# The seam between two layers: the last block's norm, its residuals, and the tensors and pools that layer 1 waits for

## The chip, the core and the metric

The kernel runs on one core of one Trainium2 chip. Its time is the device time of one execution in microseconds (us). The engines named here are PE (TensorE: matmuls, and PEld, its weight loads), DVE (VectorE), ACT (ScalarE), POOL (GpSimd) and SP (SyncE, which only issues DMAs). Each engine works through its own instructions in order and waits on semaphores for the others. A DMA is issued from SP's, POOL's or ACT's queue and lands later.

## The reference

Two residual layers on x of shape (4, 64, 256, 256), float32. `_gn` is a group norm of 32 groups without weights.

```python
    def _L0_conv_ref(x, w1, w_dw, w_out, ln_w, ln_b):
        hidden = jnp.einsum('bchw,oc->bohw', x, w1)
        hidden = jax.lax.conv_general_dilated(hidden, w_dw, window_strides=(1, 1), padding='SAME', feature_group_count=w_dw.shape[0], dimension_numbers=('NCHW', 'OIHW', 'NCHW'))
        q, k, v = jnp.split(hidden, 3, axis=1)
        qf = jnp.fft.rfft2(_to_patches(q))
        kf = jnp.fft.rfft2(_to_patches(k))
        out = jnp.fft.irfft2(qf * kf, s=(P, P))
        ...
        mu = out.mean(axis=1, keepdims=True)
        var = out.var(axis=1, keepdims=True)
        out = (out - mu) / jnp.sqrt(var + 1e-05) * ln_w[None, :, None, None] + ln_b[None, :, None, None]
        out = v * out
        return jnp.einsum('bchw,oc->bohw', out, w_out)

    def _L1_conv_ref(features, w_ih, w_hh, b_ih, b_hh):
        ...
        def step(prev_col, cur_col):
            nb = jnp.concatenate([pad, prev_col, pad], axis=1)
            x = jnp.concatenate([nb[:, :-2], nb[:, 1:-1], nb[:, 2:]], axis=-1)
            new = _gru_cell(x.reshape(B * H, 3 * Cf), cur_col.reshape(B * H, Cf), w_ih, w_hh, b_ih, b_hh).reshape(B, H, Cf)
            return (new, new)
        ...

    x = x + _L0_conv_ref(_gn(x), L0_conv_w1, L0_conv_w_dw, L0_conv_w_out, L0_conv_ln_w, L0_conv_ln_b)
    x = x + _L1_conv_ref(_gn(x), L1_conv_w_ih, L1_conv_w_hh, L1_conv_b_ih, L1_conv_b_hh)
```

Layer 0 mixes 8x8 patches by a circular convolution of q and k, takes a layer norm over the channels, multiplies with v and projects back. Layer 1 is a recurrence from image column to image column: a GRU cell whose input is the last column and whose state is the current one. Its group norm needs statistics over the whole of layer 0's result.

## The kernel before

Layer 0 goes through the image in `NBLK` = 32 blocks (line 617), eight to an image, each of 32 columns of the transposed image: block n belongs to image n // 8 and to columns 32 * (n % 8) to 32 * (n % 8) + 31. A block runs in stages: the pointwise product into `h` for one chunk of channels (16 units), `circular` (transform, products, inverse into `z`), a second chunk and `circular`, a third chunk, and `values` (k = 0 to 7, into `v`). The matrices `t` of the transforms are streamed from DRAM on SP's queue through four buffers (`fetch`, line 334). TensorE's results pass through a ring of eight PSUM banks (`psum`, line 220).

What follows on a block (norm, gate, projection, residual) is done beside the next block's TensorE work. `layer_norm` (line 472) is a generator, moved on by `go()`: statistics of `z` on DVE, the standard deviation on ACT, then eight scalings of `z` on DVE (`scaled`, for four slices of 32 features a subtraction of the mean and a multiplication with its reciprocal deviation), then eight transposes on DVE, of `z` and `v` by turns (`turned`). `gated` (line 527) takes one slice of 32 features: weight and bias of the norm on ACT, the product with `v` on POOL. `project(n, u)` (line 551) multiplies half u of the pixels with `w_out` on TensorE, four groups b of which each needs one slice. `residual(n, u)` (line 540) loads the matching part of x from DRAM to `wk` slots 6 and 2 with four DMAs on SP's queue, `add_residual` adds on DVE, and `leave` (line 579) takes statistics (`bn_stats`, after half 1 also the aggregate into `st1`) on DVE and stores the result to the DRAM tensor `x1` with four DMAs on POOL's queue.

For the last block there is no next one. At `n == NBLK` (line 620) the generator runs to its end, the four slices are gated, and for each half in turn come residual, project, add and leave. Both halves use the same slots of `wk`, so half 1's load waits for half 0's stores.

Then layer 1 begins. Its constants go to a pool `l1c` (line 730). `norm_of_blocks` (line 109) makes four means and deviations from `st1`, with two small matmuls for the sums over channels, in a short-lived pool `stb`; from them comes `sc1` (line 745), in two layouts, for even and odd columns. `load_column(w)` (line 773) loads column w of `x1` for all images to one of 16 buffers `raw`; 16 columns are loaded ahead on SP's queue. `normalize(w, slot)` of layer 1 (line 787) makes `xn` from `raw` and `sc1` on ACT and a copy `xt` with the halves exchanged on POOL. Eight of these, for columns 0 to 3, stand ahead of the first column's matmuls, and POOL then clears the edges of the state tile `st`, which the first taps read.

Pools of layer 0 lie in this order: `xp` (four buffers `xq`), `big` (`h`, `z`, `v`, `wk` and small tiles), `tp` (four `t`). They are given back when layer 0 ends, and layer 1's pools lie where they lay. A new pool's first use waits for the old one's last. Every instruction passes through one helper (`InOrder.run`, line 158), so the profile's line is L158 for nearly all; the groups are told apart by tiles and shapes.

Of the kernel before, what the change touches and what calls it, by code (L numbers as in the profile page):

```python
# [9 lines left out]
F32 = mybir.dt.float32  # L10
# [98 lines left out]
def norm_of_blocks(nc, tmp, pool, psum, mv, eps, avg4):  # L109
# [3 lines left out]
    mean = pool.tile([P, NPAIR], F32, tag="gn1_mean", name="gn1_mean")  # L113
    rstd = pool.tile([P, NPAIR], F32, tag="gn1_rstd", name="gn1_rstd")
    m_all = tmp.tile([P, NBLK], F32, tag="m_all", name="m_all")
    d = tmp.tile([P, NBLK], F32, tag="d_all", name="d_all")
    m4 = tmp.tile([P, B], F32, tag="m4", name="m4")
    nc.vector.tensor_copy(m_all, mv[:, :, 0])
    nc.vector.tensor_reduce(
        m4, m_all.rearrange("p (b n) -> p b n", n=n), mybir.AxisListType.X, ALU.add  # L120
# [6 lines left out]
        m_all.rearrange("p (b n) -> p b n", n=n),  # L127
# [5 lines left out]
    v4 = tmp.tile([P, B], F32, tag="v4", name="v4")  # L133
# [4 lines left out]
    nc.vector.reciprocal(v4, v4)  # L138
    for b in range(B):
        at = slice((b % 2) * C, (b % 2) * C + C)  # L140
        nc.vector.tensor_copy(mean[at, b // 2 : b // 2 + 1], m4[at, b : b + 1])
        nc.vector.tensor_copy(rstd[at, b // 2 : b // 2 + 1], v4[at, b : b + 1])
    return mean, rstd
# [20 lines left out]
def tile_conv_then_gru(  # L164
# [20 lines left out]
    x1 = dram.tile([B, C, W, H], F32, tag="x1", name="x1")  # L185
# [27 lines left out]
    with layer0 as s:  # L213
        big = s.enter_context(tc.tile_pool(name="big", bufs=1))
# [11 lines left out]
        hx = big.tile([P, P * NP], F32, tag="h", name="h")  # L226
# [245 lines left out]
        def layer_norm(n):  # L472
# [31 lines left out]
            def scaled(i):  # L504
                f = slice(32 * i, 32 * i + 32)
                for part, what in ((mean, ALU.subtract), (rstd, ALU.mult)):
                    nc.vector.tensor_tensor(
                        z[:, :, f],
                        z[:, :, f],
                        part.rearrange("p (n x) -> p n x", x=1).to_broadcast([P, NJ, 32]),  # L510
                        what,
                    )
                    yield

            def turned(of, i):
                chunk = of[:, :, 32 * i : 32 * i + 32]
                nc.vector.transpose(chunk, chunk)

            for i in range(4):
                yield from scaled(i)  # L520
            for i in range(4):
                turned(z, i)
                yield
                turned(v, i)
                yield

        def gated(n, i):
            f = slice(32 * i, 32 * i + 32)
            nc.scalar.activation(
                z[:, :, f],  # L530
                z[:, :, f],
# [4 lines left out]
            nc.gpsimd.tensor_tensor(v[:, :, f], v[:, :, f], z[:, :, f], ALU.mult)  # L536
# [3 lines left out]
        def residual(n, u):  # L540
            b, r0 = n // 8, (n % 8) * 32 + u * 8
            xr = [wk[:, i].rearrange("p (r c) -> p r c", c=P) for i in (6, 2)]
# [36 lines left out]
        def leave(n, u, xr):  # L579

            b, r0 = n // 8, (n % 8) * 32 + u * 8
            if u == 0:
                bn[n] = big.tile([P, 8, 6], F32, tag="bn", name=f"bn_{n}")
            for g in range(2):
# [3 lines left out]
                for s in range(2):  # L588
                    nc.gpsimd.dma_start(
                        x1[b, :, r0 + 16 * g : r0 + 16 * g + 8, s * P : s * P + P],  # L590
# [26 lines left out]
        for n in range(NBLK + 1):  # L617
            last = n == NBLK
            more = not last and n // 8 + 1 < B
            if last:  # L620
                for _ in norm:
                    pass
                for i in range(4):
                    gated(n - 1, i)
                for u in range(2):
                    xr = residual(n - 1, u)
                    add_residual(u, project(n - 1, u), xr)
                    leave(n - 1, u, xr)
# [54 lines left out]
            for unit in range(16):  # L683
# [13 lines left out]
                if unit % 4 == 3 and n + 1 < NBLK:  # L697
                    load(n + 1, unit // 4)
            po = project(n - 1, 1) if n else None
# [4 lines left out]
            for k in range(8):  # L704
# [12 lines left out]
                if k == 5 and n:  # L717
                    leave(n - 1, 1, xr[1])
                if k == 5 and n + 1 < NBLK:
                    normalize(n + 1, 3)  # L720
                if k in (6, 7):
# [18 lines left out]
    with tc.tile_pool(name="stb", bufs=1) as stb, tc.tile_pool(name="gnps1", bufs=1, space=PSUM) as gnps:  # L740
        avg4 = stb.tile([P, P], F32, tag="avg4", name="avg4")
        nc.scalar.dma_start(avg4, avg2)
        mean1, rstd1 = norm_of_blocks(nc, stb, l1c, gnps, st1, eps, avg4)
# [231 lines left out]
```

## Time and profile before

| what | value |
|---|---|
| median of 3 runs | 5094.03 us |
| lowest and highest | 5087.31, 5103.36 us |
| the profiled execution's own time | 5097.92 us |
| its span | 5096.1 us |
| mean granted TensorE clock | 0.993 |
| DVE, ACT, POOL busy | 79%, 65%, 34% of the span |
| layer 0's last values (PE) begin | 3657.29 us |
| layer 1's first tap matmul | 3735.32 us |

A row of the timeline gives start, duration, engine, line, operation, what it writes and reads, partitions x elements and, in brackets, the engine's idle time before it and what ended it. Rows of equal kind that follow each other are put together (x4). Consecutive instructions of one engine can overlap a little at their ends.

### The profile page before, as it was taken

What the parts mean: (1) busy time and instruction counts of PE and PEld (TensorE: products, weight loads), DVE (VectorE), ACT (ScalarE), POOL (GpSimd) and SP (SyncE); (2) the same over time, 40 slices, a digit from 0 to 9 for tenths busy, and PEclk for the clock granted to TensorE, in tenths of its full rate; (3) what the DMA queues carried; (4) which work ended last, traced back from release to release, by engine and by line L of the source; (5) the groups of instructions that cost most, each with busy time, mean ns of one, the idle gap of its engine ahead of it and who ended that gap; (6) DMA issues with size and microseconds to landing.
All of it is one profiled execution on the core that took longest, in us unless ns stands there. A gap on an engine that the chain in (4) does not pass through costs nothing.

```text
span 5096.1 us, 276113 instructions
## 1 busy us (share of the span) xinstructions
PE 4858.1 (95%) x127092; PEld 4237.7 (83%) x127092; DVE 4035.9 (79%) x7001; ACT 3317.3 (65%) x4269; POOL 1727.2 (34%) x1717
## 2 busy tenths in 40 slices
PE   6999999999999999999999999999879999999999
PEld 4888888888888888888888888888669999999998
DVE  5788888877888888788888877778867777777777
ACT  4666666666666666666666666666556666666665
POOL 0233333333333334333333333323343333333333
PEclk9999999999999999999999999999989999999999
DMA  8577676676777667677676666666443333333332
GB/s 306 162 189 191 186 191 182 180 183 187 187 195 196 170 184 187 179 190 191 186 195 168 173 161 174 173 171 180 121 125 103 104 103 103 102 104 103 103 103 73
DMA packets 435056, 823.57 MB, mean 162 GB/s; under 512 B 37156, under 2 KB 300068, under 8 KB 431364
## 3 DMA queue, kind: packets, MB, share of 16 engines
q1 hardware_dynamic: 380600, 582.13, 43.3%
q0 software_dynamic: 52432, 223.12, 14.7%
q8 instruction: 997, 16.33, 1.4%
q14 instruction: 163, 1.34, 0.1%
q10 hardware_dynamic: 864, 0.66, 0.0%
HBM read 660.53 MB, written 145.23 MB: 158 GB/s over the span
## 4 chain that ended last, share of the span: by engine, by line
PE 87%; ACT 4%; issue 4%; DVE 3%; DMA 2%; POOL 1%; SPq 0%; POOLq 0%; ACTq 0%; DVEq 0%
PE psring L158 62%; PE pshr L158 9%; PE pshz L158 8%; PE psni L158 6%; PE pshn L158 2%; ACT v L158 1%; ACT z L158 1%; DVE wk L158 1%; ACT xq L158 1%; DMA t<-t_all 1%; DVE z L158 1%; DMA t_all<-wk 0%; DVE lnst L158 0%; ACT h L158 0%; POOL v L158 0%
## 5 line engine op out<-in xcount | busy, mean ns | idle before, releaser
L158 PEld LDWEIGHTS psring<-h,t 100*32 100x32 f32 x49152 | 1385.9, 119 | 251.6 <-issue 214.5
L158 PE MATMUL psring<-h,t 100*32 100x128 f32 x49152 | 1463.5, 257 | 104.2 <-issue 69.4
L158 PEld LDWEIGHTS psring<-w_sb,xq 64*100 64x100 f32 x24576 | 1358.6, 163 | 107.9 <-issue 76.5
L158 PE MATMUL psring<-w_sb,xq 64*100 64x128 f32 x24576 | 1412.4, 271 | 23.0 <-issue 8.7
L158 ACT COPY h<-psring 100x1024 f32<-100x1024 f32 (+2 forms) x1371 | 1231.5, 990 | 308.0 <-PE psring L158 307.4
L158 DVE TENSOR_TENSOR wk<-psring,wk 128x1024 f32<-128x1024 f32 (+1 forms) x768 | 759.5, 1037 | 480.1 <-PE psring L158 346.4
L158 POOL TENSOR_TENSOR v<-v,z 128x2048 f32<-128x2048 f32 x128 | 582.9, 4558 | 664.5 <-DVE wk L158 603.5
L158 DVE TENSOR_TENSOR z<-z,moments 128x2048 f32<-128x2048 f32 x256 | 578.0, 2278 | 2.3
L158 POOL TENSOR_TENSOR wk<-wk 128x1024 f32<-128x1024 f32 x128 | 303.5, 2371 | 622.3 <-DVE wk L158 607.9
L158 POOL TENSOR_TENSOR raw<-raw,st 128x512 f32<-128x512 f32 x256 | 303.2, 1184 | 540.1 <-DVE st L158 424.6
L158 ACT COPY z<-psring 128x2048 f32<-128x2048 f32 (+1 forms) x144 | 248.4, 1725 | 343.9 <-PE psring L158 262.6
L158 ACT ACTIVATE z<-pshz,b_rz 128x288 f32<-128x288 f32 (+7 forms) x510 | 242.1, 475 | 339.2 <-PE pshz L158 334.1
L158 ACT COPY wk<-psring 128x1024 f32<-128x1024 f32 (+1 forms) x272 | 268.9, 988 | 288.5 <-PE psring L158 237.1
L158 PE MATMUL pshr<-st,wi 64*64 64x144 f32 (+7 forms) x12240 | 448.8, 270 | 6.9 <-DVE st L158 6.5
L158 PE MATMUL pshz<-st,wi 64*64 64x144 f32 (+7 forms) x12240 | 444.2, 269 | 0.9 <-issue 0.9
L158 PE MATMUL psni<-st,wi 64*64 64x144 f32 (+7 forms) x12240 | 444.0, 269 | 0.1
L158 DVE COPY h<-psring 100x1024 f32<-100x1024 f32 (+1 forms) x230 | 278.1, 1210 | 191.9 <-PE psring L158 188.1
L158 PEld LDWEIGHTS pshr<-st,wi 64*64 64x64 f32 x12240 | 378.0, 133 | 49.7 <-DVE st L158 36.9
L158 ACT COPY v<-psring 128x2048 f32<-128x2048 f32 (+2 forms) x176 | 251.9, 1436 | 254.3 <-PE psring L158 254.3
L158 DVE BATCH_NORM_STATS2 lnst<-z 128x6 f32<-128x128 f32 x2048 | 416.8, 281 | 0.0
L158 PEld LDWEIGHTS psni<-st,wi 64*64 64x64 f32 x12240 | 389.4, 133 | 21.9 <-issue 0.2
L158 PE MATMUL psring<-wk,g_sb 32*64 32x512 f32 x6144 | 386.7, 599 | 15.1 <-issue 12.1
(91 smaller groups left out, 6258.4 us busy)
## 6 DMA issues: line engine op xcount, KB each, us to landing
t<-t_all SPq DMA_DIRECT2D x768, 448.0 KB, 4.6
xq<-in_xh POOLq DMA_DIRECT2D x124, 800.0 KB, 5.2
wk<-in_x SPq DMA_DIRECT2D x256, 256.0 KB, 8.1
x<-wk POOLq DMA_DIRECT2D x256, 256.0 KB, 5.0
wk<-in_x POOLq DMA_DIRECT2D x96, 512.0 KB, 6.9
raw<-x SPq DMA_DIRECT2D x128, 256.0 KB, 3.0
raw<-x SPq DMA_DIRECT2D x256, 128.0 KB, 3.1
out<-raw SPq DMA_DIRECT2D x128, 256.0 KB, 2.7
```

The costliest lines, as they stand in the source:

```text
L158: return self.tc.keep_in_program_order(got(*args, **kwargs))
```

## The change

The last block's norm is shared: `scaled` takes an engine, and slices 2 and 3 of block 31 are scaled on POOL, slices 0 and 1 on DVE. Its transposes go by halves of the pixels (32 of 64), its gates too, and each half is projected once its four slices are gated; the product of the last slice of half 1 is on DVE. Both halves are added, then both leave. The residuals of block 31 are loaded beside block 31's own third chunk: half 0 to `wk` slots 1 and 5, half 1 to slots 6 and 2 after block 30's last stores, which go out on SP's queue instead of POOL's. The generator isn't moved on at k = 6 and 7 of the last block. `x1` becomes eight DRAM tensors of 32 columns each. `h` gets a pool of its own, `hp`, between `xp` and `big`. `norm_of_blocks` uses tiles of `l1c` in place of `stb`, leaves out a copy and builds `sc4` for all images at once, from which four copies make `sc1`; a Sigmoid of one element per partition follows its Sqrt on ACT.

```diff
-def norm_of_blocks(nc, tmp, pool, psum, mv, eps, avg4):
+def norm_of_blocks(nc, tmp, psum, mv, eps, avg4, sc):
...
     n = NBLK // B
-    mean = pool.tile([P, NPAIR], F32, tag="gn1_mean", name="gn1_mean")
-    rstd = pool.tile([P, NPAIR], F32, tag="gn1_rstd", name="gn1_rstd")
-    m_all = tmp.tile([P, NBLK], F32, tag="m_all", name="m_all")
     d = tmp.tile([P, NBLK], F32, tag="d_all", name="d_all")
     m4 = tmp.tile([P, B], F32, tag="m4", name="m4")
-    nc.vector.tensor_copy(m_all, mv[:, :, 0])
+    v4 = tmp.tile([P, B], F32, tag="v4", name="v4")
     nc.vector.tensor_reduce(
-        m4, m_all.rearrange("p (b n) -> p b n", n=n), mybir.AxisListType.X, ALU.add
+        m4, mv[:, :, 0].rearrange("p (b n) -> p b n", n=n), mybir.AxisListType.X, ALU.add
     )
...
         d.rearrange("p (b n) -> p b n", n=n),
-        m_all.rearrange("p (b n) -> p b n", n=n),
+        mv[:, :, 0].rearrange("p (b n) -> p b n", n=n),
         m4.rearrange("p (b x) -> p b x", x=1).to_broadcast([P, B, n]),
...
     nc.vector.tensor_tensor(d, d, mv[:, :, 1], ALU.add)
-    v4 = tmp.tile([P, B], F32, tag="v4", name="v4")
     nc.vector.tensor_reduce(v4, d.rearrange("p (b n) -> p b n", n=n), mybir.AxisListType.X, ALU.add)
...
     nc.scalar.activation(v4, pv, AF.Sqrt, bias=eps, scale=1.0)
-    nc.vector.reciprocal(v4, v4)
-    for b in range(B):
-        at = slice((b % 2) * C, (b % 2) * C + C)
-        nc.vector.tensor_copy(mean[at, b // 2 : b // 2 + 1], m4[at, b : b + 1])
-        nc.vector.tensor_copy(rstd[at, b // 2 : b // 2 + 1], v4[at, b : b + 1])
-    return mean, rstd
+    nc.scalar.activation(d[:, 0:1], eps, AF.Sigmoid, bias=eps, scale=1.0)
+    nc.vector.reciprocal(sc[:, :, 1], v4)
+    nc.vector.scalar_tensor_tensor(sc[:, :, 0], m4, -1.0, sc[:, :, 1], ALU.mult, ALU.mult)
...
     dram = ctx.enter_context(tc.tile_pool(name="dram", bufs=1, space=DRAM))
-    x1 = dram.tile([B, C, W, H], F32, tag="x1", name="x1")
+    x1 = [dram.tile([B, C, 32, H], F32, tag=f"x1_{i}", name=f"x1_{i}") for i in range(W // 32)]
...
     with layer0 as s:
+        hp = s.enter_context(tc.tile_pool(name="hp", bufs=1))
         big = s.enter_context(tc.tile_pool(name="big", bufs=1))
...
-        hx = big.tile([P, P * NP], F32, tag="h", name="h")
+        hx = hp.tile([P, P * NP], F32, tag="h", name="h")
         h = hx[0:HALO].rearrange("p (c n) -> p c n", n=NP)
...
-            def scaled(i):
+            def scaled(i, engine=nc.vector):
                 f = slice(32 * i, 32 * i + 32)
                 for part, what in ((mean, ALU.subtract), (rstd, ALU.mult)):
-                    nc.vector.tensor_tensor(
+                    engine.tensor_tensor(
                         z[:, :, f],
...
-            def turned(of, i):
-                chunk = of[:, :, 32 * i : 32 * i + 32]
+            def turned(of, i, n0=0, n1=NJ):
+                chunk = of[:, n0:n1, 32 * i : 32 * i + 32]
                 nc.vector.transpose(chunk, chunk)
-            for i in range(4):
+            if n < NBLK - 1:
+                for i in range(4):
+                    yield from scaled(i)
+                for i in range(4):
+                    turned(z, i)
+                    yield
+                    turned(v, i)
+                    yield
+                return
+            for i in (2, 3):
+                for _ in scaled(i, nc.gpsimd):
+                    pass
+            for i in (0, 1):
                 yield from scaled(i)
-            for i in range(4):
-                turned(z, i)
-                yield
-                turned(v, i)
-                yield
-
-        def gated(n, i):
+            for u in range(2):
+                for i in range(4):
+                    turned(z, i, 32 * u, 32 * u + 32)
+                    turned(v, i, 32 * u, 32 * u + 32)
+                    yield
+
+        def gated(n, i, n0=0, n1=NJ, engine=nc.gpsimd):
             f = slice(32 * i, 32 * i + 32)
             nc.scalar.activation(
-                z[:, :, f],
-                z[:, :, f],
+                z[:, n0:n1, f],
+                z[:, n0:n1, f],
                 AF.Identity,
...
             )
-            nc.gpsimd.tensor_tensor(v[:, :, f], v[:, :, f], z[:, :, f], ALU.mult)
+            engine.tensor_tensor(v[:, n0:n1, f], v[:, n0:n1, f], z[:, n0:n1, f], ALU.mult)
...
-        def residual(n, u):
+        def residual(n, u, at=(6, 2)):
             b, r0 = n // 8, (n % 8) * 32 + u * 8
-            xr = [wk[:, i].rearrange("p (r c) -> p r c", c=P) for i in (6, 2)]
+            xr = [wk[:, i].rearrange("p (r c) -> p r c", c=P) for i in at]
             for g in range(2):
...
-        def leave(n, u, xr):
-
-            b, r0 = n // 8, (n % 8) * 32 + u * 8
+        def leave(n, u, xr, queue=nc.gpsimd):
+
+            b = n // 8
             if u == 0:
...
                 for s in range(2):
-                    nc.gpsimd.dma_start(
-                        x1[b, :, r0 + 16 * g : r0 + 16 * g + 8, s * P : s * P + P],
+                    queue.dma_start(
+                        x1[n % 8][b, :, u * 8 + 16 * g : u * 8 + 16 * g + 8, s * P : s * P + P],
                         xr[g][s * C : (s + 1) * C],
...
             if last:
-                for _ in norm:
-                    pass
-                for i in range(4):
-                    gated(n - 1, i)
+                po = []
                 for u in range(2):
-                    xr = residual(n - 1, u)
-                    add_residual(u, project(n - 1, u), xr)
-                    leave(n - 1, u, xr)
+                    for i in range(4):
+                        go()
+                        gated(n - 1, i, 32 * u, 32 * u + 32, nc.vector if u and i == 3 else nc.gpsimd)
+                    po.append(project(n - 1, u))
+                for u in range(2):
+                    add_residual(u, po[u], xrs[u])
+                for u in range(2):
+                    leave(n - 1, u, xrs[u])
                 break
...
                     load(n + 1, unit // 4)
+            if n == NBLK - 1:
+                xrs = [residual(n, 0, (1, 5))]
             po = project(n - 1, 1) if n else None
...
                 if k == 5 and n:
-                    leave(n - 1, 1, xr[1])
+                    if n < NBLK - 1:
+                        leave(n - 1, 1, xr[1])
+                    else:
+                        leave(n - 1, 1, xr[1], nc.sync)
+                        xrs.append(residual(n, 1))
                 if k == 5 and n + 1 < NBLK:
                     normalize(n + 1, 3)
-                if k in (6, 7):
+                if k in (6, 7) and n < NBLK - 1:
                     go()
...
     nc.vector.tensor_scalar(b_rz[:, 1:2], b_rz[:, 1:2], -1.0, None, ALU.mult)
-    with tc.tile_pool(name="stb", bufs=1) as stb, tc.tile_pool(name="gnps1", bufs=1, space=PSUM) as gnps:
-        avg4 = stb.tile([P, P], F32, tag="avg4", name="avg4")
+    with tc.tile_pool(name="gnps1", bufs=1, space=PSUM) as gnps:
+        avg4 = l1c.tile([P, P], F32, tag="avg4", name="avg4")
         nc.scalar.dma_start(avg4, avg2)
-        mean1, rstd1 = norm_of_blocks(nc, stb, l1c, gnps, st1, eps, avg4)
+        sc4 = l1c.tile([P, B, 2], F32, tag="sc4", name="sc4")
+        norm_of_blocks(nc, l1c, gnps, st1, eps, avg4, sc4)
         sc1 = l1c.tile([P, 2, NPAIR, 2], F32, tag="sc1", name="sc1")
-        nc.vector.scalar_tensor_tensor(sc1[:, 0, :, 0], mean1, -1.0, rstd1, ALU.mult, ALU.mult)
-        nc.vector.tensor_copy(sc1[:, 0, :, 1], rstd1)
-        for slot in range(2):
+        for way in range(2):
             for half in range(2):
-                b = SLOTS[1][slot][half]
+                b0, step = SLOTS[way][0][half], SLOTS[way][1][half] - SLOTS[way][0][half]
                 nc.vector.tensor_copy(
-                    sc1[half * C : (half + 1) * C, 1, slot], sc1[(b % 2) * C : (b % 2) * C + C, 0, b // 2]
+                    sc1[half * C : (half + 1) * C, way],
+                    sc4[half * C : (half + 1) * C, b0 : b0 + step + 1 : step],
                 )
...
-            raw = raws[w]
+            raw, at = raws[w], w % m.shape[2]
             if w % 2 == 0:
-                yield m[:, :, w, :].rearrange("(k a) c h -> (a c) k h", k=NPAIR), raw
+                yield m[:, :, at, :].rearrange("(k a) c h -> (a c) k h", k=NPAIR), raw
             else:
...
                     b0 = SLOTS[1][0][half]
-                    yield m[b0 : b0 + 2, :, w, :].rearrange("b c h -> c b h"), raw[half * C : half * C + C]
+                    yield m[b0 : b0 + 2, :, at, :].rearrange("b c h -> c b h"), raw[half * C : half * C + C]
...
             raws[w] = rawp.tile([P, 2, H], F32, tag="raw", name=f"raw_{w}")
-            for of, to in column_parts(x1, w):
+            for of, to in column_parts(x1[w // 32], w):
                 nc.sync.dma_start(to, of)
```

## The prediction

> **What bounds the kernel now.** I read the page's busy times first. TensorE works for 95% of the span, so only a stretch where it doesn't work can shrink much.
>
> ```profile
> span 5096.1 us, 276113 instructions
> ...
> PE 4858.1 (95%) x127092; PEld 4237.7 (83%) x127092; DVE 4035.9 (79%) x7001; ACT 3317.3 (65%) x4269; POOL 1727.2 (34%) x1717
> ```
>
> Then the busy time by stage, around the place where layer 0 ends and layer 1 begins (length, then busy time and count by engine, granted clock, DMA share, GB/s).
>
> ```profile
> 3640.00:3657.00 17.00, 16.84 (x304) 12.65 (x300) 12.10 (x45) 11.67 (x13) 1.26 (x1) 1.00 0.37 82
> 3657.00:3677.00 20.00, 16.45 (x520) 15.54 (x512) 19.90 (x16) 6.50 (x5) 2.78 (x4) 1.00 0.80 200
> 3677.00:3732.00 55.00, 13.12 (x132) 3.94 (x132) 34.24 (x52) 11.39 (x10) 24.11 (x14) 0.57 0.32 77
> 3745.00:3800.00 55.00, 54.10 (x1717) 49.43 (x1721) 42.06 (x103) 39.50 (x90) 24.10 (x41) 1.00 0.38 112
> ```
>
> In 3677 to 3732 TensorE works 13.1 of 55 us; on both sides it is full. All that the change touches lies there or just before it. The timeline of that stretch (start, duration, engine, work, and in brackets the idle time before and what ended it):
>
> ```profile
> 3670.73 9.08 DVE L158 TENSOR_TENSOR z<-z,moments 128x2048 f32<-128x2048 f32 x4
> 3679.73 2.30 DVE L158 STREAM_TRANSPOSE z<-z 128x2048 f32<-128x2048 f32 x1
> ...
> 3684.40 4.45 POOL L158 TENSOR_TENSOR v<-v,z 128x2048 f32<-128x2048 f32 x1 [21.22 <-DVE v L158]
> ...
> 3702.41 5.93 PE L158 MATMUL psring<-v,wo_sb 32*64 32x512 f32 x80 [2.40 <-POOL v L158]
> ...
> 3709.57 4.47 SPq L158 DMA_DIRECT2D wk<-in_x  x4
> 3715.95 1.29 DVE L158 TENSOR_TENSOR wk<-psring,wk 128x512 f32<-128x512 f32 x2 [6.66 <-DMA wk<-in_x]
> ...
> 3719.53 2.46 DVE L158 BATCH_NORM_STATS2 bn<-wk 128x6 f32<-128x512 f32 x4
> ...
> 3722.03 0.37 DVE L158 BATCH_NORM_AGGREGATE st<-bn 128x2 f32<-128x48 f32 x1
> ...
> 3730.38 4.25 ACT L158 ACTIVATE xn<-raw,sc 128x256 f32<-128x256 f32 x8 [4.70 <-DMA raw<-x]
> ...
> 3734.64 1.28 ACT L158 ACT_TABLE_LOAD   x1
> ```
>
> The reader sees one chain: DVE scales z until 3679.7, eight transposes until 3697.4, POOL's four products (4.42 apart) until 3702.4, the projection until 3708.3, a late residual until 3719.6, statistics, layer 1's norm, a load of x1, and ACT's first xn at 3730.38. Layer 1 begins with that xn, so I follow it.
>
> **The change, part by part.** Two of four scalings of z go to POOL, beside DVE's two. Each of these has two inputs in SBUF, on both engines, and no row has this pair side by side. The nearest pair is in layer 1, column by column:
>
> ```profile
> 3840.19 0.42 DVE L158 SCALAR_TENSOR_TENSOR g<-z,xn 128x250 f32<-128x250 f32 x1 [0.56 <-ACT z L158]
> 3840.58 0.57 DVE L158 TENSOR_TENSOR n<-n,z 128x250 f32<-128x250 f32 x1
> 3841.18 0.42 DVE L158 TENSOR_TENSOR st<-n,g 128x250 f32<-128x250 f32 x1
> ...
> 3840.19 0.68 POOL L158 COPY xt<-xn 64x256 f32<-64x256 f32 x1
> 3841.46 0.40 POOL L158 COPY xt<-xn 64x256 f32<-64x256 f32 x1 [0.59 <-ACT xn L158]
> ```
>
> The POOL copy that starts with DVE's g takes 0.68 instead of 0.40, and DVE's next takes 0.57 instead of 0.42: they take turns. The four-product row next to transposes (one input) shows no such thing: 2.27 with POOL busy, 2.30 without. So the cost of the overlap lies between nothing (both at full speed) and full turns (the sum of both). I take full turns, because the 0.28 that the copy loses is most of the 0.40 it could lose.
>
> The Trainium skill speaks against this part too: "SBUF — State Buffer", section "Who interferes with whom", says that a VectorE instruction with two SBUF inputs and a GpSimd one that reads SBUF exclude each other for a whole instruction. The rows above show it for 0.4 us instructions only; a split of bandwidth would fit them as well. By the page this part costs full turns, by a 5% loss as in the mean of all xt copies (412 ns against a least of 392) almost nothing: 18 us of gain in place of 9.
>
> Step by step, in the old trace's time. The mean is ready at 3656.2 (TENSOR_SCALAR moments, 3655.99 and 0.20); POOL follows 0.17 later (as its first product follows the transpose that ends at 3684.23), ahead of DVE's first at 3656.7, which waits for the reciprocal. Four POOL products at 4.45 (the v<-v,z row) and four DVE ones at 2.28 make 17.8 + 9.1 = 26.9 in turns: both end at 3683.2. The four adds of the block before read PSUM and fit in DVE's waits; they end some 4 us later than 3661.3 and hold back the values' PSUM banks as long, so the last copy of v ends near 3682 instead of 3678.1, still ahead of its transpose. Then bn_stats of block 30 (2.46) and aggregate (0.3): 3686.0, against 3679.7 before. **A loss of 6.3.**
>
> From here halves. A half transpose: at least 1.10 (half the step of 2.19), at most 1.25 with a fixed part; I take 1.13. First pair done 3688.3, ACT's half (1.1, half of 2.09 and a little) lies beside the second, POOL starts at 3688.4. A half product on POOL lies between 2.21 (half of 4.42) and 2.56 (raw<-raw,st at its slowest, 1.28 for 512); I take 2.37, the row wk<-wk 128x1024, which has its size. Seven: 16.6, so 3705.0. The transposes stay ahead (the sixteenth at 3704.1). The eighth product goes to DVE, two inputs again, so after POOL's seventh: 3705.0 to 3706.2. The last two groups of the projection take some 2 us each at the low clock (2.02 in the old rows of 16): 3708.9. From the first transpose to here that is 22.9 us, and was 28.6 (3679.73 to 3708.34): **a gain of 5.7.**
>
> **Residuals early.** Residual 31,0 goes to wk 1 and 5 and is issued on SP behind residual 30,1 (3634.97), once the last inverse has read them (3642.6). Its four DMAs (3.8 us of SP) push one t load from 3638.8 to 3646.5, needed at 3663: hidden. Block 30's last four stores move from POOL (2.78, which would queue behind the 17.8 of scaling) to SP, behind the last t load (3665.7, or 4 later with the held values), and residual 31,1 follows their landing (4.9), near 3678 instead of 3709.57. It lands 6.5 later, the adds need it at 3708.9: 24 us of cover. Without it the 6.66 + 1.09 of idle DVE would be back. The adds take 2.48 behind the projection, 3711.4, where 11.3 passed before: **a gain of 8.8.** But both halves' bn_stats now stand behind both adds, 4.92 instead of 2.46, until 3716.3: **a loss of 2.5.**
>
> **Norm and loads.** The norm loses one copy (0.2) and nine small ones; from aggregate to the square root 3.45, so 3719.8. Then reciprocal, one multiply and four copies: 3720.8 instead of 2.1 later. The Sigmoid now brings the table load (1.28 and 0.29, the row moments<-eps) in front of xn: 3721.4; it costs 0.6 there. Before, the load cost nothing, since the next sigmoid waited for TensorE until 3736.74. From aggregate to xn 5.1, where 8.35 passed (3722.03 to 3730.38), 2.6 of them for the first raw load: **a gain of 3.3.**
>
> The skill's "ScalarE: Activation LUTs", section "What ACT_TABLE_LOAD costs", gives 2.66 us for a switch with its drain, an estimate of 1.1 more than mine; no row here shows a drain.
>
> The raw loads need only x1's first tensor and h's pool. Both are free once the values end (about 3680): behind residual 31,1, 24 issues at 0.67 are over at 3698, so xn waits for no load. Loads from the other seven tensors, and their shorter rows' pitch, cost nothing: a load lands in 3 us and is sent 16 columns of 5.3 us ahead. Stores of block 31 stay on POOL: 8 at 0.7, the last near 3713.9, landed 4.9 later at 3718.8, 2.6 ahead of xn, should its tiles still wait for the work pool. From xn to the first tap 4.9 as before (eight POOL copies, then the memset).
>
> Sum: 6.3 - 5.7 - 8.8 + 2.5 - 3.3, so xn at 3721.4 instead of 3730.4, **9.0 us less**. The profiled execution took 5097.92 (span 5096.1 and 1.8 around it), so 5088.9; it stood 3.9 above the median 5094.03. For the median: **5085**.
>
> **Rivals.**
> **No turns**: the two engines run beside each other. DVE reaches the transposes at 3670.7 (the old row, with two scalings fewer behind it), POOL ends at 3674.2; ACT is held by the last copy of v until 3678.1, so POOL's halves run from 3679.3 to 3695.9 instead of 3705.0; 18.1 less, **5076**. For it: 412 against 392 ns. Against it: the five rows above. Between the two: if DVE has the first turn, POOL's last scaling ends at 3683.5 with everything behind it ready, and its halves at 3700.1, 4.9 earlier: 5080.
> **Loads late**: layer 1's tiles wait for the whole work pool in spite of the new pool. Loads go out at 3718.8 and xn follows 3.5 later (3726.87 to 3730.38), at 3722.3: **5086**. For it: before, the first load went out at 3726.9, after the last store. Against it: the first 16 raw buffers (32 KB) fit in xq's and h's 89 KB.
> **POOL slow on a repeated operand** (the other side): moments is one number repeated over 32 columns, which no POOL row has. Below: 3.1 (one input, 0.39 for 256), above: twice, 8.9. Every us above 4.45 counts four times; the kernel is slower than before from 6.7 on, and at 8.9 it takes **5103**. Against it: DVE shows 2.28 with and 2.30 without a repeated operand.
>
> **How the numbers follow.** Full turns 0.48, no or cheap turns 0.35, loads late 0.07, POOL slow 0.10. A measurement of this kernel tells 0.3% (15 us) from no change, so faster means below 5078.7. Full turns alone give 5078 to 5092 (POOL's order +-5, its half product and table load +-2.5, spread of a median +-4); of that 0.22 falls below the bound, and of the second case 0.75: 0.11 + 0.26 = 0.37. Slower: 0.06 from slow POOL, 0.01 else. The range takes in no turns with its spread, and the start of slow POOL: 5072 to 5096.
>
> **What would show it.** DVE's z<-z,moments of the last block: 2.28 if there are no turns, up to 6.7 with waiting if there are. POOL's four: the last ends near 3681 to 3683, or 3674. First raw load: about 3680. Idle DVE in front of the last adds: for TensorE only. xn: 3721. I am wrong if the raw loads stay behind the stores, if SP holds the t loads back so that the values end after 3686, or if layer 1 changes its pace (its 256 columns took 1360 us from 3735; 1% there would be more than all this).

## The result, and the profile after

The kernel after takes 5082.67 us (median of 20 runs, 5073.34 to 5096.32), the kernel before on the same chip 5094.49 us (20 runs, 5087.31 to 5111.31). The ratio estimated from these runs is 0.9972, 95% interval 0.9964 to 0.9981 (the quotient of the two medians alone is 0.9977): faster, by 10 to 18 us, which is well under 1%. The profiled execution of after is the slowest of its 20 (5096.32 us), so the two spans differ by 1.6 us only.

```profile
span 5094.5 us, 276119 instructions
...
PE 4872.0 (96%) x127092; PEld 4243.5 (83%) x127092; DVE 4035.3 (79%) x6996; ACT 3319.8 (65%) x4274; POOL 1741.5 (34%) x1720
```

Whole spans hide what happened here, because layer 0 ahead of the change varies by itself. I set a zero point: the last TENSOR_SCALAR of `moments` on DVE, where block 31's mean is ready. It stands at 3655.99 us in the trace before and at 3666.09 after, 10.1 later, ahead of nearly all that the change does. Counted from there, the first tap matmul of layer 1 (PE pshr<-st,wi) comes at 79.34 us before and at 65.89 us after: **13.45 us gained at the seam**. The stages of after (length, busy time and count by engine, granted clock, DMA share, GB/s):

```profile
3655.00:3667.00 12.00, 12.00 (x224) 9.95 (x224) 10.60 (x43) 8.51 (x10) 0.57 (x1) 1.00 0.65 133
3667.00:3687.00 20.00, 16.21 (x528) 15.30 (x512) 19.96 (x8) 7.21 (x5) 19.84 (x4) 1.00 0.54 148
3687.00:3729.00 42.00, 12.96 (x133) 3.50 (x134) 36.95 (x55) 13.92 (x16) 22.41 (x19) 0.66 0.67 165
3742.00:3797.00 55.00, 55.00 (x1761) 49.56 (x1756) 43.01 (x106) 40.15 (x92) 24.39 (x42) 1.00 0.36 102
```

The stage in which TensorE idles is 42 us long in place of 55, and holds the same 13 us of TensorE work. POOL's time in the stage ahead of it rose from 2.78 to 19.84: the four scalings. The timeline rows of after for the chain that the prediction followed:

```profile
3666.43 3.64 POOL L151 TENSOR_TENSOR z<-z,moments 128x2048 f32<-128x2048 f32 x1 [15.09 <-DVE moments L151]
3666.79 5.43 DVE L151 TENSOR_TENSOR z<-z,moments 128x2048 f32<-128x2048 f32 x1
3670.15 5.57 POOL L151 TENSOR_TENSOR z<-z,moments 128x2048 f32<-128x2048 f32 x1
3674.54 14.62 DVE L151 TENSOR_TENSOR z<-z,moments 128x2048 f32<-128x2048 f32 x3
3691.87 1.19 DVE L151 STREAM_TRANSPOSE z<-z 128x1024 f32<-128x1024 f32 x1
3694.41 16.02 POOL L151 TENSOR_TENSOR v<-v,z 128x1024 f32<-128x1024 f32 x7 [7.39 <-ACT z L151]
3710.12 1.38 DVE L151 TENSOR_TENSOR v<-v,z 128x1024 f32<-128x1024 f32 x1 [0.18 <-ACT z L151]
3711.43 4.86 DVE L151 TENSOR_TENSOR wk<-psring,wk 128x512 f32<-128x512 f32 x8
3716.22 4.83 DVE L151 BATCH_NORM_STATS2 bn<-wk 128x6 f32<-128x512 f32 x8
3721.07 0.37 DVE L151 BATCH_NORM_AGGREGATE st<-bn 128x2 f32<-128x48 f32 x1
3724.53 1.28 ACT L151 ACT_TABLE_LOAD   x1
3727.25 4.04 ACT L151 ACTIVATE xn<-raw,sc 128x256 f32<-128x256 f32 x8 [1.13 <-DMA raw<-x]
```

Three things are to be seen. DVE's scaling takes 5.43 beside POOL's, where it took 2.28 alone; POOL's first takes 3.64 and the next, which waits for DVE, 5.57. From the first transpose to the aggregate DVE hardly idles: the wait of 6.66 us for a late residual, which stood in front of the second adds before, is gone. And xn does not follow the norm directly: 1.13 us pass that the profile puts down to a DMA.

### The profile page after: what moved, and what is told of

The parts are those of the page before. It is cut to its first block, busy times and chain, and to the rows that moved or that the text cites. A ratio compares the mean times of both kernels' runs of the same rounds, so it can differ in the third digit from the quotient of the medians.

```text
span 5094.5 us, 276119 instructions
## 1 busy us (share of the span) xinstructions
PE 4872.0 (96%) x127092; PEld 4243.5 (83%) x127092; DVE 4035.3 (79%) x6996; ACT 3319.8 (65%) x4274; POOL 1741.5 (34%) x1720
## 4 chain that ended last, share of the span: by engine, by line
PE 87%; ACT 4%; issue 4%; DVE 3%; DMA 2%; POOL 0%; SPq 0%; POOLq 0%; ACTq 0%; DVEq 0%
PE psring L151 62%; PE pshr L151 9%; PE pshz L151 8%; PE psni L151 6%; PE pshn L151 2%; ACT v L151 1%; ACT z L151 1%; DMA t<-t_all 1%; DVE wk L151 1%; DVE z L151 1%; ACT xq L151 1%; DMA t_all<-z 1%; SPq L151 0%; ACT h L151 0%; DVE n L151 0%
## 5 line engine op out<-in xcount | busy, mean ns | idle before, releaser
L151 POOL TENSOR_TENSOR v<-v,z 128x2048 f32<-128x2048 f32 (+1 forms) x131 | 581.3, 4442 | 644.0 <-DVE wk L151 602.6
```

Of the source, the lines that this page charges most:

```text
L151: return self.tc.keep_in_program_order(got(*args, **kwargs))
```

## The experiments

Each kernel was compared with the kernel before, run beside it on the same chip. The kernel before took 5095.12 us beside e1 to e4, 5077.87 beside e5 to e8 and 5074.76 beside e9 and e10 (medians), so of the whole times only the ratios compare. Since the seam repeats far better than the whole, both are given. Kernels that differ only elsewhere repeat the same rows to some 0.01 us: POOL's last product ends at 44.33 or 44.34 in after, in e2, e4, e6 and e7.

| kernel | zero point (us) | first tap after it | first sigmoid g after it | ratio to before, 95% |
|---|---|---|---|---|
| before | 3655.99 | 79.34 | 80.75 | 1 |
| after | 3666.09 | 65.89 | 68.12 | 0.9972 (0.9964 to 0.9981) |
| e1, scaling on DVE alone | 3655.48 | 63.65 | 65.87 | 0.9969 (0.9957 to 0.9982) |
| e2, avg loaded on SP | 3659.82 | 64.66 | 66.88 | 0.9973 (0.9963 to 0.9983) |
| e3, scaling in sequence | 3653.68 | 61.25 | 62.75 | 0.9961 (0.9945 to 0.9977) |
| e4, residuals late | 3664.62 | 73.02 | 75.11 | 0.9996 (0.9986 to 1.0006) |
| e5, no halves | 3641.99 | 71.84 | 73.70 | 0.9992 (0.9983 to 1.0001) |
| e6, one tensor x1 | 3636.38 | 65.54 | 67.48 | 0.9961 (0.9948 to 0.9975) |
| e7, h in the work pool | 3642.62 | 66.89 | 68.05 | 0.9977 (0.9965 to 0.9988) |
| e8, e3 + e2, no Sigmoid | 3639.02 | 59.20 | 61.97 | 0.9956 (0.9943 to 0.9968) |
| e9, e8 + Sigmoid behind xn | 3634.13 | 59.18 | 60.78 | 0.9969 (0.9956 to 0.9981) |
| e10, e8 + Sigmoid as in after | 3645.01 | 59.74 | 61.88 | 0.9968 (0.9956 to 0.9980) |

**e1: does sharing the scaling gain anything by itself?** All four slices go back to DVE; all else stays.

```diff
-            for i in (2, 3):
-                for _ in scaled(i, nc.gpsimd):
-                    pass
             for i in (0, 1):
                 yield from scaled(i)
+            for i in (2, 3):
+                for _ in scaled(i):
+                    pass
```

> All eight scalings of the last block back on DVE, all else as changed. Measured by the seam: from the start of the last TENSOR_SCALAR on moments to the first tap matmul (pshr<-st,wi); 79.33 us in the kernel before, 65.90 in the changed one. Theory (turns): beside POOL, DVE's four scalings took from 3666.79 to 3689.16 with the adds inside; eight alone take 8 x 2.25 + 2.47 of adds, 2 us less until the transposes begin, and all behind is bound by DVE: seam 63.9. Rival (sharing spares DVE work): seam longer by up to the 9.1 us of four scalings, 68 to 75.

Measured: tap at 63.65. The eight scalings of e1, in the timeline (three of the first four, then the other four):

```profile
3660.70 6.81 DVE L151 TENSOR_TENSOR z<-z,moments 128x2048 f32<-128x2048 f32 x3
...
3670.22 9.08 DVE L151 TENSOR_TENSOR z<-z,moments 128x2048 f32<-128x2048 f32 x4
```

Alone they take 2.28 each again, and the transposes begin at 23.75 us after the zero point instead of 25.77. So the sharing, as the change does it, is a loss of 2.24 us at the tap. Turns are shown by this pair: the same instruction on the same data takes 2.28 us without POOL beside it and 3.33 to 5.72 with it. A split of the bandwidth between the two would have slowed POOL's first scaling as well; in after it takes 3.64, what POOL takes alone in e3 below, and DVE's, begun 0.36 later, ends 2.15 behind it.

**e3: the same scalings on POOL, but not at the same time.** DVE scales slices 0 and 1 alone; POOL scales 2 and 3 behind it (a copy of one element waits for DVE), beside DVE's transposes of slices 0 and 1. A second edit goes with it: DVE takes all four products of slices 2 and 3, three of them POOL's in after.

```diff
+            for i in (0, 1):
+                yield from scaled(i)
+            nc.gpsimd.tensor_copy(spare[:, 0, 0:1], z[:, NJ - 1, 63:64])
             for i in (2, 3):
                 for _ in scaled(i, nc.gpsimd):
                     pass
-            for i in (0, 1):
-                yield from scaled(i)
...
+                    for i in (2, 3):
+                        times(n - 1, i, 32 * u, 32 * u + 32, nc.vector)
...
```

> POOL's four scalings wait (by a one-element copy) for DVE's four; meanwhile DVE does adds, statistics and the transposes of slices 0 and 1, which have one SBUF input; POOL takes the products of slices 0 and 1, DVE those of slices 2 and 3. Theory (turns): no turns while scaling, POOL's four in 4 x 3.64 = 14.6 us, DVE's in 9.1; transposes end some 10 us earlier, products with some turns between POOL and DVE end near 3706 in place of 3711.5 of the changed kernel's time: seam 60 to 62.5. Rival (POOL is slow whatever stands beside it, 5.1 us each as in the changed kernel): POOL ends 6 us later, seam 65 to 68.

Measured: tap at 61.25, 4.64 less than after. The groups of e3 that write z (count, then shortest, median and longest in ns):

```profile
L151 DVE TENSOR_TENSOR z<-z,moments x4: 2228/2285/2292, 3654.4 to 3663.4; 128x2048 f32<-128x2048 f32 x4
L151 POOL TENSOR_TENSOR z<-z,moments x4: 3636/3638/3642, 3666.0 to 3677.0; 128x2048 f32<-128x2048 f32 x4
```

All four of POOL's now take 3.64, beside transposes and statistics on DVE, which keep their pace (a half transpose 1.20 as in after). Only the pair of two-input instructions takes turns. It is seen once more where DVE's products meet POOL's: the first two take 2.37 and 3.34, the last two, behind POOL's last, 1.21. Of the 4.64, 3.40 is there at the aggregate (51.58 us after the zero point, 54.98 in after); the rest is a wait of xn for stores, which e2 explains and e3 doesn't have. Against DVE alone (e1, aggregate at 53.08) e3 gains 1.5. So POOL's help is worth having where DVE does something with one input; how much of it the moved products bring was not separated.

**e4: the residuals as before the change**, loaded when they are needed, and each half leaves before the next is added.

```diff
-            if n == NBLK - 1:
-                xrs = [residual(n, 0, (1, 5))]
...
                 for u in range(2):
-                    add_residual(u, po[u], xrs[u])
-                for u in range(2):
-                    leave(n - 1, u, xrs[u])
+                    xr = residual(n - 1, u)
+                    add_residual(u, po[u], xr)
+                    leave(n - 1, u, xr)
...
-                        xrs.append(residual(n, 1))
```

> Block 31's residuals are loaded after the projections again, both to wk 6 and 2, and each half adds and leaves in turn. Theory (residual on the path): half 0's load is early enough, half 1's waits for half 0's stores (landing near 3719 of the changed kernel's time), lands near 3726, its adds end 12 us later, half 0's statistics lie in that wait: seam 75.5, up to 85 if the raw loads go ahead of it on SP. Rival (loads hidden by the halves anyway): seam 65.9 to 68.

Measured: 73.02 at the tap, 7.13 worse than after, where I had expected 75.5. On the timeline of e4 the stall of before is back in front of the adds:

```profile
3715.05 4.50 SPq L151 DMA_DIRECT2D wk<-in_x  x4
...
3721.65 1.29 DVE L151 TENSOR_TENSOR wk<-psring,wk 128x512 f32<-128x512 f32 x2 [6.84 <-DMA wk<-in_x]
...
3732.92 4.02 ACT L151 ACTIVATE xn<-raw,sc 128x256 f32<-128x256 f32 x8
```

Of the parts undone one at a time, the early residual is the largest. Up to the aggregate it is worth 8.37 (63.35 against 54.98); 1.2 of it returns, since in e4 ACT goes on to xn without idle time, 4.95 behind the aggregate, where after takes 6.18.

**e5: transposes, gates and products of whole slices**, all four products on POOL, both projections behind them.

```diff
-            for u in range(2):
-                for i in range(4):
-                    turned(z, i, 32 * u, 32 * u + 32)
-                    turned(v, i, 32 * u, 32 * u + 32)
-                    yield
+            for i in range(4):
+                turned(z, i)
+                turned(v, i)
+                yield
...
+                for i in range(4):
+                    go()
+                    gated(n - 1, i)
...
```

> The last block's transposes, gates and products whole again (all four products on POOL), both projections behind them; sharing, early residuals, tensors and pools as changed. Theory (the halves start POOL earlier and let the projection and the adds of half 0 lie beside POOL): transposes begin 25.8 us behind the start of the seam as in the changed kernel, POOL's four products of 4.42 end at 50.1, both projections at 56, the second adds at 58.5, the aggregate begins at 63.3 instead of 54.98: seam 73.5 to 74.5. Rival (DVE sets the pace, so POOL's order matters little): seam 66 to 68.

Measured: 71.84, 5.95 worse than after. That is below the 73.5 to 74.5 of the theory, but far from the rival's 66 to 68: halves are worth about 6 us. Up to the aggregate the loss is 7.2 (62.15 against 54.98); 1.2 of it returns since xn no longer waits for a store (landed at 64.34, xn at 67.12).

**e6: one DRAM tensor x1 instead of eight.**

```diff
-    x1 = [dram.tile([B, C, 32, H], F32, tag=f"x1_{i}", name=f"x1_{i}") for i in range(W // 32)]
+    x1 = dram.tile([B, C, W, H], F32, tag="x1", name="x1")
...
```

> x1 is one DRAM tensor again; the pool for h stays. The raw loads then wait for block 31's last store. Theory (xn waits for those stores in any case, since its tiles lie where the work tiles lay, and avg's late load holds most raw loads back): the stores land at 57.8 with no loads beside them instead of 60.7, the first raw load lands some 3 later, xn at 61.4 instead of 61.16: seam 66.2, no more than 0.5 from the changed kernel's 65.89. Rival (the early loads save the 2.6 us wait of the kernel before): seam 68.5 or more.

Measured: 65.54, 0.35 better than after. The mechanism that I named is refuted. On e6's timeline the loads go out early all the same, 27.13 us after the zero point, in after 27.11:

```profile
3663.51 34.90 SPq L151 DMA_DIRECT2D raw<-x  x24
```

Here a load of other columns doesn't wait for block 31's stores, even in one tensor. So the eight tensors bring nothing. The 0.35 is the last store's landing, 60.35 us after the zero point against 60.70 in after; why it lands earlier stays open.

**e7: h back in the work pool.**

```diff
-        hp = s.enter_context(tc.tile_pool(name="hp", bufs=1))
...
-        hx = hp.tile([P, P * NP], F32, tag="h", name="h")
+        hx = big.tile([P, P * NP], F32, tag="h", name="h")
```

> h is a tile of the pool big again; x1 stays in eight tensors. Theory (a new pool waits for all of an old one that it lies on): the raw buffers lie partly on big, so their loads wait for the stores' landing as with one x1: seam 66.2, the same as with one x1, within 0.3. Rival (a buffer waits only for the tile that it lies on): loads as early as in the changed kernel, first raw load at 27, seam 65.9 with the gap behind the seventh load as before.

Measured: 66.89, 1.0 worse than after (0.7 more than expected). The loads now wait for the last store: it lands 57.82 us after the zero point and the first raw load goes out at 58.26 (at 27.11 in after). xn follows 3.54 later, at 61.80. The stores land 2.9 earlier than in after (60.70), with no loads beside them. So h's own pool takes the load off the path and puts a collision in its place; the net is 1 us at the tap. At the first g nothing of it is left (68.05 in e7, 68.12 in after): e7's taps happened to meet the full clock, after's half of it, as the last section shows.

**e2: which wait split the raw loads?** In after the 24 loads were to follow each other at 0.67. SP's queue shows another picture (three rows of the timeline, the last one POOL's):

```profile
3690.39 2.73 SPq L151 DMA_DIRECT2D wk<-in_x  x4
3693.21 34.93 SPq L151 DMA_DIRECT2D raw<-x  x24
...
3713.00 5.49 POOL L151 DMA_DIRECT2D x<-wk  x8 [2.58 <-DVE wk L151]
```

34.93 us for 24 issues; the eighth goes out at 3711.25, 12.9 after the seventh. What SP's queue waited for between 3690 and 3730, in after (us in total, times, longest):

```profile
SPq L151 <- DMA avg<-in_avg: 12.5, 1, 12.5
SPq L151 <- DVE bn L151: 7.9, 1, 7.9
```

The loads don't read avg. ACT issues avg's load at 3709.27, behind its last gate. In the trace's records avg's load counts on a semaphore that SP's loads and stores use too, and the eighth raw load waits for just that semaphore. The seventeen loads that were held then went out together with block 31's eight stores. The stores took 7.9 us to land (median), against 5.9 in e2 below, where the last raw load lands 3.0 us after the first store goes out. The last landed at 3726.80, and xn began 0.45 later. In e1 and e6 xn also begins 0.46 behind that landing, though the loads that the first xn read had all landed by 3703 in after. So the row's "DMA raw<-x" is the last of several waits; the one that counts here is for the stores, whose tiles lie where layer 1's `xn` was put. e2 issues avg on SP, ahead of the raw loads:

```diff
-        nc.scalar.dma_start(avg4, avg2)
+        nc.sync.dma_start(avg4, avg2)
```

> The 64 KB load of avg moves from ACT's queue to SP's, behind the biases. Theory (one counter): the ninth raw load waits 12.5 us for avg's landing, which ACT issues only behind its last gate; the loads that are held back then meet block 31's stores, which land after 8 us instead of 5, and xn waits 1.1 us for them since its tiles lie where the work tiles lay. So all raw loads go out in one run from 3693 on, the stores land in some 5 us, xn starts right behind the Sigmoid: seam 64.8. Rival (raw loads are held by a pool or by their buffers): the gap of 12.5 us stays, seam 65.9.

Measured: 64.66, 1.23 better than after, as expected. In e2 the loads go out in one run, 0.75 each, xn follows the Sigmoid without idle time, and the last store lands 2.9 earlier, 57.84 us after the zero point:

```profile
3687.60 17.98 SPq L151 DMA_DIRECT2D raw<-x  x24
```

**e8: what is left if all that was found is put right.** e3's sequence, e2's queue, the Sigmoid of the norm left out, and each half leaves before the other is added.

```diff
-        nc.scalar.dma_start(avg4, avg2)
+        nc.sync.dma_start(avg4, avg2)
...
-    nc.scalar.activation(d[:, 0:1], eps, AF.Sigmoid, bias=eps, scale=1.0)
...
```

> The scalings in sequence as in the run of that name, avg's load on SP, no Sigmoid ahead of xn, and half 0 leaves (statistics and stores) before half 1 is added. Theory: from the seam of 61.25 of the sequence alone, 1.4 less for DVE's wait ahead of the second adds, in which half 0's statistics now lie, and 0.45 less for xn that waited for the Sigmoid: 59.4; the table load then lies behind the eight xn and ends before the first taps do, so costs nothing. In time some 20 us less than the kernel before. Rival (the stores' landing takes over as the last wait, since xn's tiles lie on the work tiles): no gain over 61.25; rival (the table load then delays the first sigmoid): tap as in the theory, but layer 1 ends 1 us later after it.

Measured: tap at 59.20 (expected 59.4), 6.7 less than after; 0.9956 (0.9943 to 0.9968) of before. But without the Sigmoid the table load comes back, on e8's timeline directly in front of the first g and behind its wait for TensorE:

```profile
3699.70 1.28 ACT L150 ACT_TABLE_LOAD   x1 [2.17 <-PE pshr L150]
3700.99 0.50 ACT L150 ACTIVATE g<-pshr,b_rz 128x288 f32<-128x288 f32 x1
```

**e9 and e10: where should the table load stand?** e9 puts a Sigmoid of one element behind the eight xn, e10 leaves it behind the norm's Sqrt, both on top of e8.

```diff
                 normalize(w, slot)
+        warm = l1c.tile([P, 1], F32, tag="warm", name="warm")
+        nc.scalar.activation(warm, eps, AF.Sigmoid, bias=eps, scale=1.0)
         empty_states(0)
```

> The kernel with the three edits (scaling in sequence, avg's load on SP, no Sigmoid in the norm), and in addition a Sigmoid of one element per partition on ACT behind the eight xn. Nothing else. In the kernel without it the table load (1.28 us) stands directly in front of the first g, behind g's wait for TensorE: tap at 59.20 us after the last moments, g at 61.97, 2.77 later. Theory: that load lies on the path, and ACT idles for 2.2 us in front of it, so it is hidden behind the xn: tap unchanged (59.2 +-0.2), g 1.28 earlier (60.7 +-0.3), from tap to g 1.5. Rival: g waits for TensorE's taps, which run slowly here at the low clock, and the load is hidden in any case: g at 61.7 to 62.0.

> The same two edits (scaling in sequence, avg's load on SP) with the Sigmoid left where the change put it, behind the norm's Sqrt. Theory: the table load (1.28 + 0.29 us) then stands in front of the first xn, which waited 0.95 us for sc without it, so xn, copies and tap come 0.7 us later (tap 59.9 +-0.3) but g has no load in front of it: g at 61.4 +-0.3, 0.6 earlier than the 61.97 without the Sigmoid and 0.7 later than with the Sigmoid behind the xn. Rival (the load costs nothing in front of g): g at 62.5 or later.

Measured: e9's tap is unchanged at 59.18 and g comes at 60.78, 1.19 earlier than in e8. The load now lies in ACT's idle time, on e9's timeline:

```profile
3692.63 1.28 ACT L150 ACT_TABLE_LOAD   x1
...
3694.91 0.50 ACT L150 ACTIVATE g<-pshr,b_rz 128x288 f32<-128x288 f32 x1 [0.69 <-PE pshr L150]
```

So the load lay on the path in e8: the theory of e9 holds. In e10 the tap came at 59.74, as expected, but g at 61.88 and not at 61.4: 2.14 after the tap, in e9 1.60. What differs between them is the granted clock, the number behind the counts, in e10 and then in e9, over the 2 us that begin near the tap:

```profile
3704.50:3706.50 2.00, 2.00 (x37) 1.84 (x34) 0.00 (x0) 0.00 (x0) 1.31 (x6) 0.50 0.04 8
```

```profile
3693.00:3695.00 2.00, 2.00 (x49) 1.84 (x46) 0.00 (x0) 1.30 (x3) 1.36 (x6) 0.75 0.00 0
```

The same taps run at 0.50 in e10 and at 0.75 in e9.

By the seam e9 is the best version: 20.0 us less than before to the first g, 7.3 less than after. By the whole time e8, e9 and e10 can't be told apart, and none of them is shown to be faster than after: their intervals overlap with its own.

## Why the prediction was right, and where its steps were off

The time (5085, measured 5082.67) and the likeliest case, full turns, were right. That the time came out only 2.3 us off is in part luck: at the seam the sum was 4.4 off, and the kernel's runs spread over 23 us. The range (5072 to 5096) also held no turns at all (5076) and no change (5094), so it is the rows, and not the time, that tell the cases apart. The median did not fall below 5078.7, which the prediction named as its bound for faster; with 20 runs of each kernel the interval still leaves out no change. The terms of the sum, in us, a loss with a minus (the last column has the length of each step):

| step | predicted | measured | from which rows |
|---|---|---|---|
| scaling, until the first transpose | -6.3 | -2.03 | 23.74 before, 25.77 after |
| halves, until the projection ends | +5.7 | +6.71 | 28.61 before, 21.90 after |
| residual early, until the adds end | +8.8 | +8.76 | 11.28 before, 2.52 after |
| both statistics behind both adds | -2.5 | -2.37 | 2.41 before, 4.78 after |
| norm and loads, until xn | +3.3 | +2.17 | 8.35 before, 6.18 after |
| xn to the first tap | 0 | +0.22 | 4.95 before, 4.73 after |
| sum | 9.0 | 13.45 | |

**The scaling was mis-sized, by 4.3.** The step "four POOL products at 4.45 (the v<-v,z row)" took a product of two full operands for the scaling, whose second operand is one number repeated over 32 columns. POOL takes 3.64 for it. That is 3.2 less for four; the other 1.0 is overlap at the seven turns (a DVE row ends 2.14 to 2.15 behind POOL's, a POOL row 3.50 to 3.51 behind DVE's, each 0.13 to 0.14 less than alone). 22.73 us passed from POOL's first scaling to DVE's last, where the sum of the rows alone is 4 x 3.64 + 4 x 2.28 = 23.7 and the prediction had 26.9.

**Full turns** hold. The rows behind it were one pair of 0.4 us instructions; e1 and e3 show it for 2 to 6 us. The Trainium skill's "SBUF — State Buffer", section "Who interferes with whom", which I weighed against a split of bandwidth, agrees with the measurement: 3.33 to 5.72 beside POOL and 2.28 alone, and no loss where DVE has one input in SBUF. The rival **no turns** has fallen with it.

**POOL slow on a repeated operand** has fallen, and to the other side: it is faster, 3.64 against 4.45. I had bounded this cost from 3.1 to 8.9 and then taken the full product's 4.45 for want of a row. The "2.30 without a repeated operand" for DVE is a transpose's row, with one input, so it said nothing on this; in e3 a DVE product of two full operands takes 1.21 for half the size once POOL is done.

**Halves**: the rows were near (seven products in 16.02, predicted 16.6; transposes 1.125 apart, predicted 1.13). Undone alone they are worth 7.2 up to the aggregate and 5.95 at the tap (e5).

**Residuals early**: 8.76 and 2.37, as worked out; undone alone 8.4 up to the aggregate and 7.1 at the tap (e4), where the two terms give 6.4. Residual 31,1 waited for DVE's statistics of block 30 (7.9 us of SP's queue) until 3690.39, 24.3 after the zero point and 2.3 later than predicted; the cover of 24 us took it.

**Norm and loads**: here a step was wrong and not only a size. "24 issues at 0.67 are over at 3698, so xn waits for no load" missed the wait for avg, and "the last near 3713.9, landed 4.9 later" missed what it brings: the loads collide with the stores, and the tiles do still wait for the work pool. It cost 1.1 us in front of xn (1.23 by e2). The shorter norm itself came as forecast: from the aggregate to the last copy of sc 4.61 passed, 5.73 before. Of the rival **loads late**, the wait for the whole pool was seen in e7 and is worth 1.0 at the tap. "The raw loads need only x1's first tensor": they'd have needed no tensor of their own (e6).

**Table load**: the 0.6 that I put on it was hidden in after by the wait for the stores; without that wait it is 0.54 (e10's tap at 59.74, e8's at 59.20), and left out it costs 1.2 at the first g (e8 against e9). The skill's "ScalarE: Activation LUTs", section "What ACT_TABLE_LOAD costs", adds a drain of 1.38 us to each switch. No row here has it: the load of e8 ends at 3700.98 and g begins at 3700.99.

What stays open: layer 0 up to the zero point varies by more than any part here is worth (e9 and e10 share its program and differ by 10.9 us), and nothing was tried on that. Block 30's stores on SP's queue, the generator held back at k = 6 and 7 and the shorter norm were not undone one by one, so what each is worth by itself is not shown.

## What to carry to other kernels

Moving half of an elementwise step to POOL beside the same step on DVE was a loss here, where both read two tiles of SBUF; POOL's share ran at full pace while DVE transposed, took statistics or read PSUM. A load that is needed at a known time should be issued as soon as its buffer is free, and what is queued on the same completion counter should be looked at too. When the whole time is noisy, measure from a common event on both sides of the change, and take the end far enough behind it: at the first tap e7 and after differ by 1.0, at the first g by 0.07.

## What was not expected of the hardware

- POOL's product of 128x2048 float32 takes 3.64 us when the second operand is repeated over 32 columns, and 4.45 when it is a full tile.
- A DMA's wait can be for a transfer it has nothing to do with: 12.5 us for avg<-in_avg, in front of the eighth raw load, gone in e2.
- The first taps of layer 1 run at half clock for a time that differs from trace to trace. By windows of 1 us, the granted clock rises from 0.50 to 1.00 about 4.0 us after layer 1's first matmul in before, 6.0 in after, 3.6 in e7, 3.8 in e9 and 4.9 in e10. The same taps take 1.41 us until g before and 2.23 after, so 0.8 of the gain is given back there. The Trainium skill's "TensorE: Matmul & The Clock Gate", section "Part 1: The HAM clock gate (the "warmup" mystery)", says that the clock follows a free-running window of 3.4 us; a whole busy window would then be seen 3.4 to 6.8 us after the start, an estimate from that page which all five fit.
- Eight DMA stores of 256 KB land in 7.9 us (median) when seventeen loads go out beside them, and in 5.9 in e2, where the last load lands 3.0 us after the first store goes out.
